# Two graph layers: later loads of x and weights, earlier splits and transposes of x

## The chip, the core and the metric

The kernel runs on one core of a Trainium2 chip. A core has five engines that run their own instruction queues and wait for each other on semaphores: TensorE (PE, matrix products), VectorE (DVE), ScalarE (ACT), GpSimd (POOL) and SyncE (SP). Data come from memory over 16 DMA engines; POOL and SP issue these loads into a queue each. The metric is the device time in microseconds.

## What is computed

Two layers over the same 4096 x 4096 graph, whose entries are 0 or 1 with about 16 ones in a row, and 64 features:

```python
# layer 0
rank = cumsum(adj, axis=1); deg = rank[:, -1:]
k = minimum(deg, 100); pos = rank - (deg - k)
w = adj * where(pos > 0, 0.5 ** (k - pos), 0)
x = layernorm(x + w @ (x @ W0) + b0)
# layer 1
deg = maximum(sum(adj, axis=1) + 1, 1)
h = (adj @ x + x) / deg
z = relu(concatenate([x, h], axis=1) @ W + b1)      # W holds wx over wn
x = layernorm(x + z / maximum(norm(z), 1e-12))
```

Layer 0 needs, for each edge, how many edges stand to its right in its row: the weight halves with every one.

## The kernel before

**Tiles and steps.** The adjacency matrix lies transposed and is cut into 64 tiles (8 row groups g of 512 rows, 8 column pieces k of 512). `load_next` (L102 to L110) issues the load of one tile on POOL's queue, with a cast to bf16. The kernel calls it 8 times ahead of the loop and once in every step of it. A step i handles one tile, groups in order and pieces from 7 down to 0 within a group. PE counts ones by column quarters (`count`, L317; the first count of a tile is the first use of its load), DVE adds these to the counts of the pieces to the right (`cs`), PE spreads them (`spread`), ACT makes `near` of it. `weigh` (L343) then makes the 2^-rank weights by 32 small products (L351, L360) and two evictions, one by ACT (L367) and one by DVE (L368). `gather` (L373) multiplies the weights of the step before with x. The count in step i is that of tile i + 1. Sums of layer 1 over parts of x that are ready fill the later steps (L387).

**x comes twice.** `load_xp` (L122) loads x in an order that fits the tiles into the buffer `c1` (named c in the profile), in two halves: first pieces 4 to 7, then 0 to 3. `split_x` (L218) makes of piece k a high part in fp16 (by POOL, for pieces 6 and 7 by ACT) and a rest, and `split_x_low` (L225, DVE) turns the rest into the low part. `gather` reads both. For groups 2 to 6, `early_px` (L281) transposes these parts on PE, `early_xT` (L286) copies them out by ACT, and `early_pu` (L291) multiplies them with `wc_parts`. `load_x` (L126) loads x of one group in its natural order, 128 KB, and `add_b0` (L308, on POOL) adds the bias b0 to it.

**Weights.** `load_weights` (L211) loads one tile of 385 columns. Of the columns come, on POOL and PE: `prepare` (scales W0), `centered` (wx with its mean taken off, L244), `centered_parts` (L252, makes `wc_parts`), `products`, `prepare_wx`, `prepare_wn`.

**What sets the order.** The order of instructions on each engine is that of the program; no scheduler moves them. Small jobs are put on hooks: `at(i, engine, fn)` (L608) puts a job into step i, after a look into the table `PLACES` (L39), which can give another step. In step i the loop (L711 to L749) runs the jobs of ACT, then `load_next`, then those of POOL, then the tile's work, and at the end those of PE and of DVE. Jobs of one step and engine run in the order in which they were put on the hook. For this change these matter: split_x of piece k stood in the step of tile (0, k); load_weights in step 1 on DVE; load_x and add_b0 of group 0 in steps 3 and 7 on POOL; prepare in step 5, bias_columns in step 7, centered_parts in step 9 on POOL; early_px in steps 3 to 7; early_pu from step 9 on PE.

**Loads that wait on purpose.** `load_x` and `load_weights` first set one column of their target to 0 with a memset on POOL or DVE. The load, on SP's queue, has to wait for this memset; so it is issued only when that engine has come to this point. SP serves its queue in order.

**Start.** PE runs 14 products on zeros (L693) and some more on the first tile (`warm`, L696). Meanwhile DVE makes masks out of number patterns that POOL writes with iota.

Of the kernel before, what the change touches and what calls it, by code (L numbers as in the profile page):

```python
# [10 lines left out]
BF16 = mybir.dt.bfloat16  # L11
# [4 lines left out]
ALU = mybir.AluOpType  # L16
AX = mybir.AxisListType
PE = mybir.EngineType.PE
ACT = mybir.EngineType.Activation
DVE = mybir.EngineType.DVE  # L20
POOL = mybir.EngineType.Pool
SP = mybir.EngineType.SP

P = 128
# [3 lines left out]
Q = P // 4  # L28
MAX_NEIGH = 100
STEP = 128.0  # L30
# [7 lines left out]
HALVED = range(2, 7)  # L38
PLACES = {"centered_parts": (9, POOL), "prepare": (5, POOL), "bias_columns": (7, POOL), "prepare_wx": (10, POOL), "half_c1_b1 3": (38, POOL), "half_c1_b1 4": (46, POOL), "half_c1_b1 5": (57, POOL), "half_c1_b1 6": (62, POOL), "products_parts": (10, POOL), "first_mv 0": (10, "DVE, early"), "first_r 0": (11, "DVE, early"), "first_least 0": (13, "DVE, early"), "first_s 0": (11, ACT), "first_pu 0": (16, PE), "times_degree 0": (18, POOL), "first_least 1": (20, DVE), "first_pu 1": (24, PE), "first_mv 2": (28, DVE), "first_s 2": (29, ACT), "first_r 2": (29, DVE), "half_scale 2": (29, DVE), "first_x1 2": (30, POOL), "first_hi 2": (31, ACT), "first_xl 2": (31, POOL), "first_lo 2": (32, ACT), "first_least 2": (31, DVE), "half_high 2": (26, ACT), "half_rest 2": (26, DVE), "half_degree_out 2": (26, DVE), "half_degree 2": (26, PE), "half_low 2": (27, ACT), "half_pz 2": (27, PE), "half_y 2": (27, DVE), "first_x1 3": (37, POOL), "first_hi 3": (38, "ACT, late"), "first_least 3": (38, "DVE, early"), "half_low 3": (34, ACT), "half_b1 3": (38, POOL), "half_c1 3": (37, POOL), "first_s 4": (44, ACT), "half_scale 4": (45, "DVE, early"), "first_xl 4": (46, POOL), "first_least 4": (45, DVE), "first_lo 4": (47, "ACT, late"), "half_low 4": (42, ACT), "half_b1 4": (46, POOL), "first_s 5": (52, ACT), "half_scale 5": (53, DVE), "first_hi 5": (54, "ACT, late"), "first_least 5": (57, DVE), "half_low 5": (50, ACT), "half_b1 5": (52, POOL), "half_c1 5": (55, POOL), "first_s 6": (60, ACT), "first_xl 6": (62, POOL), "first_lo 6": (62, "ACT, late"), "half_low 6": (58, ACT)}  # L39
LAG = 1  # L40
SAVED = (15, 17, 18, 21, 27)


@with_exitstack
def adj_resnorm_kernel(
# [23 lines left out]
    nc = tc.nc  # L69
    D = x.shape[2]  # L70
    NG, NK = adjT.shape[0], adjT.shape[1]
# [4 lines left out]
    const = ctx.enter_context(tc.tile_pool(name="const", bufs=1))  # L76
# [13 lines left out]
    for g in range(NG):  # L90
        sizes = {3: [1, 1, 2, 2, 2], 4: [2, 2, 2, 2], 7: [2, 2, 4]}.get(g, [1] * 8 if g < 3 else [4, 4])
        k = NK
# [4 lines left out]
    when = {s: i for i, s in enumerate(steps)}  # L97
# [4 lines left out]
    def load_next(n=1):  # L102
        for _ in range(n):
            s = next(loads, None)
            if s is None:
                return
            g, k = s
            a = a16p.tile([P, KB, R], BF16, tag="a16", name=f"a16_{g}_{k}")
            nc.gpsimd.dma_start(out=a, in_=adjT[g, k])  # L109
            A[g][k] = a  # L110
# [5 lines left out]
    c1 = const.tile([P, NB, D], F32, name="c1")  # L116
    xp = c1
# [3 lines left out]

    def load_xp(k0, k1):  # L122
        bs = slice(k0 * KB, k1 * KB)
        nc.sync.dma_start(out=xp[:, bs, :], in_=x_quads[:, bs, :])

    def load_x(g):  # L126
# [3 lines left out]

    load_xp(NK // 2, NK)
    load_next()
    load_xp(0, NK // 2)
    dist = epi.tile([P, P], I32, tag="hT", name="dist")
    nc.gpsimd.iota(dist, [[1, P]], base=0, channel_multiplier=-1)
    load_next()
# [3 lines left out]
    of_m = epi.tile([P, P], I32, tag="z", name="of_m")  # L140
    nc.gpsimd.iota(of_m, [[1, 4], [4 * KB, NK], [4, KB]], base=0, channel_multiplier=-1)
    load_next(6)

    idle = epi.tile([P, R], BF16, tag="near", name="idle")
    nc.vector.memset(idle, 0.0)
# [2 lines left out]
    quarters = [slice(e * Q, (e + 1) * Q) for e in range(4)]  # L148
# [10 lines left out]
    ident = epi.tile([P, P], F32, tag="near", name="ident")  # L159
    nc.vector.tensor_scalar(ident, dist, 0.0, None, ALU.is_equal)  # L160
    cen, wcf, b0T = prep[0:D, 0:D], prep[0:D, D : 2 * D], prep[0:D, 2 * D : 4 * D]
    w32, wc32 = prep[:, 4 * D : 6 * D], prep[:, 6 * D : 7 * D]
    nc.vector.tensor_scalar(cen, ident[0:D, 0:D], -1.0 / D, None, ALU.add)


    has = epi.tile([P, P], BF16, tag="y", name="has")
    nc.vector.tensor_scalar(has, of_p, 0.0, None, ALU.is_equal)
    past = epi.tile([P, P], BF16, tag="hT", name="past")
# [9 lines left out]
        else:  # L178
            nc.vector.tensor_scalar(mine[quarters[e]], one_hot, STEP, None, ALU.mult)

    tri = const.tile([P, Q], BF16, name="tri")
    for rows in quarters:
        nc.vector.tensor_scalar(tri[rows], dist[rows, rows], 0.0, -STEP, ALU.is_lt, ALU.mult)
        nc.vector.scalar_tensor_tensor(
            tri[rows], ident[rows, rows], STEP * MAX_NEIGH, tri[rows], ALU.mult, ALU.add
        )
    most = const.tile([P, 1], F32, name="most")
    nc.vector.memset(most, MAX_NEIGH)
    less = const.tile([P, 1], F32, name="less")
# [1 line left out]


    wts = const.tile([P, 6 * D + 1], F32, name="wts")
    w0_sb, wn_sb, wx_sb, b1_sb, b0_sb, w0T_sb = [wts[:, j * D : (j + 1) * D] for j in range(6)]
    wc_parts = const.tile([P, 2, D], FP16, name="wc_parts")
    wz_parts = const.tile([P, 2, 2 * D], FP16, name="wz_parts")
    b0c = const.tile([P, D], F32, name="b0c")
# [6 lines left out]
    nc.vector.memset(power, -0.5)  # L204
    x1T = const.tile([P, R], FP16, name="x1T")
    ident16 = const.tile([P, P], FP16, name="ident16")
    nc.vector.tensor_copy(ident16, ident)
    ident_b = const.tile([P, P], BF16, name="ident_b")
    nc.vector.tensor_copy(ident_b, ident)

    def load_weights():  # L211

        nc.vector.memset(wts[:, 0:1], 0.0)
        nc.sync.dma_start(out=wts, in_=weights)

    xrs = {}

# [38 lines left out]
        nc.gpsimd.tensor_tensor(wc_parts[:, 1, :], wc32, wc_parts[:, 0, :], ALU.subtract)  # L256

    def bias_columns():
        nc.gpsimd.tensor_copy(b0T, wts[0:D, 6 * D : 6 * D + 1].to_broadcast([D, P]))

    def products():
        pw[1] = ps_m.tile([P, 2, D], F32, tag="m", name="pw_1")
# [133 lines left out]
    def ready(i, g, b):  # L396
        k = b // KB
        return i >= low_at[k] + LAG and i >= when[g, k]

# [75 lines left out]
    def first_hT(g):  # L475
        h = ep["hT", g] = epi.tile([P, R], F32, tag="hT", name=f"hT0_{g}")
        nc.scalar.copy(h, acc0[g])
# [130 lines left out]
    def at(i, engine, fn, *args):  # L608
        i, engine = PLACES.get(" ".join([fn.__name__, *map(str, args)]), (i, engine))
        hooks[i, engine].append((fn, args))  # L610

    def run(i, engine):
        for fn, args in hooks.pop((i, engine), []):
            fn(*args)

    def all_at(i, *work):
        for step, engine, fn, *args in work:
            at(i + step, engine, fn, *args)

    for k in range(NK):  # L620
        i = when[0, k]
        at(i, POOL, split_x, k)
        at(i, DVE, split_x_low, k)
    at(1, DVE, load_weights)
    at(NK - 2, POOL, prepare)
    at(NK + 1, POOL, prepare_wx)
    at(NK + 2, POOL, prepare_wn)
    for g in range(NG):
        at(NK * g + 3, POOL, load_x, g)
        at(NK * g + 7, POOL, add_b0, g)  # L630
        at(min(NK * g + 12, NS - 2), POOL, add_self, g)
    if HALVED:
        all_at(
# [7 lines left out]
            (2, POOL, products_parts),  # L641
        )
    for j, g in enumerate(reversed(HALVED)):
        all_at(j + 3, (0, PE, early_px, g), (1, ACT, early_xT, g))
        all_at(NK + 1 + j, (0, PE, early_pu, g), (0, DVE, early_xw, g))
    for g in range(NG - 1):
        i = NK * (g + 1)
# [42 lines left out]


    pi = ps_a.tile([P, R], F32, tag="acc1", name="pi")
    for i in range(14):  # L693
        nc.tensor.matmul(pi, lhsT=idle[:, 0:P], rhs=idle, start=True, stop=True)

    def warm(n):  # L696

        a = A[0][NK - 1][:, 0, :]
        for i in range(n):
            nc.tensor.matmul(pi, lhsT=a[:, 0:P], rhs=a, start=True, stop=True)  # L700
# [3 lines left out]
    further = const.tile([P, P], BF16, name="further")  # L704
    nc.vector.tensor_copy(further, pf)
    count(0, NK - 1, True, True)
    warm(4)
    spread(0, NK - 1)
    warm(2)
    held = None  # L710
    for c, chunk in enumerate(chunks):  # L711
        ahead = chunks[c + 1] if c + 1 < len(chunks) else []

        shares = [[]] * (len(chunk) - 1) + [ahead]
        nr = near[chunk[0][0]]
        for (g, k), share in zip(chunk, shares):
            i = when[g, k]
            run(i, ACT)
            load_next()
            run(i, POOL)  # L720

            w = weigh(g, k, nr) if i == 0 else None
            for s in share:
                count(*s, s == ahead[0], s == ahead[-1])
            run(i, "DVE, early")
            w = w or weigh(g, k, nr)
            run(i, "ACT, late")
            if i == 0:
                warm(4)
            n_todo = len(todo)  # L730
            done = some_sums(i, 0 if i in SAVED else QUOTA)
            half = 0
            if share and share[-1] == ahead[-1]:
                if held is not None and len(todo) == n_todo:

                    half = KB // 2
                    gather(*held, 0, half)
                spread(*ahead[-1])
            if i == 0:
                warm(3)  # L740
            if done is not None:
                evict_part(done)
            if held is not None:
                gather(*held, half)
            held = (g, k, w)
            if g > 0 and k == NK - 1:
                first_hT(g - 1)
            run(i, PE)
            run(i, DVE)  # L749
# [318 lines left out]
```

## Time and profile before

| what | value |
|---|---|
| median of 3 runs | 234.12 us (233.64 to 234.18) |
| the profiled execution | 233.72 us |
| its span, first to last instruction | 231.7 us |
| PE busy | 209.5 us, 90% |
| DVE busy | 182.2 us, 79% |
| ACT busy | 140.6 us, 61% |
| POOL busy | 112.3 us, 48% |
| adjacency tiles on POOL's queue | 64, 512 KB written each |
| landing of a tile after its issue, median | 15.2 us |
| the first tile: issue, first count | 1.23 us, 8.94 us |
| weights: issue on SP | 18.57 us |
| first natural piece of x: issue on SP | 20.80 us |
| first product with wc_parts | 38.21 us |

```profile
PE   7589999998998999999999999999999999999910
...
PEclk9799999999999999999999999999999999999975
DMA  6999999999999999999999999999970000000013
```

Each digit is the busy share of one of 40 slices of the span, 5.8 us each, in tenths. PEclk is the clock that TensorE was granted, in tenths of full speed. The DMA engines are full from the second slice to the thirtieth (174 us); after that PE works off what is loaded, and the last slices are small operations and stores. A line of the timeline has start, length, engine, source line, operation, output and inputs, and in brackets how long the engine stood idle before it and what ended that.

### The profile page before, as it was taken

The numbers are of one execution on the slowest core, as the hardware profiler recorded it, in microseconds if no ns is written. First come the engines' busy times: TensorE is split into PE (matmuls) and PEld (weight loads), VectorE is DVE, ScalarE is ACT, GpSimd is POOL, SyncE is SP. The second block draws the span as 40 slices with busy tenths as digits, with TensorE's granted clock in tenths as the row PEclk, the third lists the DMA queues.
The fourth block names the chain that finished last, engine by engine and source line by source line (L and its number), as shares of the span: only waits on it lengthen the run. The fifth ranks groups of instructions, "written<-read, shape, count | busy, mean of one in ns | idle before, by whom it ended". The sixth has DMA issues, their size and how long they took to land.

```text
span 231.7 us, 7494 instructions
## 1 busy us (share of the span) xinstructions
PE 209.5 (90%) x3138; PEld 95.2 (41%) x3178; DVE 182.2 (79%) x454; ACT 140.6 (61%) x212; POOL 112.3 (48%) x211
## 2 busy tenths in 40 slices
PE   7589999998998999999999999999999999999910
PEld 2133445443533443334333433443334344776810
DVE  6459877997797789798975996687678866599983
ACT  6057886687778767686557455664675451142684
POOL 7439677761537081641584056325433040079970
PEclk9799999999999999999999999999999999999975
DMA  6999999999999999999999999999970000000013
GB/s 201 209 213 219 215 216 213 217 217 214 215 219 212 214 214 223 211 214 214 218 217 207 200 183 210 204 195 181 205 168 4 3 0 0 3 0 1 23 45 113
DMA packets 11984, 37.36 MB, mean 161 GB/s; under 512 B 1328, under 2 KB 3504, under 8 KB 11952
## 3 DMA queue, kind: packets, MB, share of 16 engines
q0 software_dynamic: 9216, 33.56, 73.7%
q1 hardware_dynamic: 2736, 3.34, 4.7%
q8 instruction: 24, 0.39, 0.6%
q14 instruction: 8, 0.07, 0.1%
HBM read 69.40 MB, written 1.05 MB: 304 GB/s over the span
## 4 chain that ended last, share of the span: by engine, by line
PE 40%; DVE 11%; POOL 4%; ACT 3%; issue 2%; ACTq 0%; DVEq 0%; POOLq 0%
PE acc L378 12%; PE acc_part L387 11%; PE v L351 5%; PE cnt L321 3%; PE v L360 3%; ACT u L961 2%; POOL scratch L947 2%; DVE w L368 2%; POOL scratch L978 2%; DVE cs L331 1%; PE rep L339 1%; PE va L930 1%; PE pz L505 1%; PE vb L387 1%; DVE part L403 1%
## 5 line engine op out<-in xcount | busy, mean ns | idle before, releaser
L367 ACT ACTIVATE w<-v,less 128x1024 int16<-128x1024 f32 x64 | 71.3, 1113 | 43.7 <-PE v L360 31.7
L368 DVE TENSOR_SCALAR w<-v 128x1024 int16<-128x1024 f32 x64 | 78.2, 1221 | 13.0 <-PE v L360 12.1
L378 PE MATMUL acc<-w,xhl 128*128 128x512 bf16 x235 | 65.2, 380 | 1.9 <-issue 1.1
L109 POOL DMA_DIRECT2D a<-in_adjT_dram x64 | 36.9, 622 | 48.2 <-PE acc_part L387 25.4
L387 PE MATMUL acc_part<-a,x1hl 128*128 128x512 bf16 x140 | 38.2, 381 | 1.8 <-issue 1.3
L378 PEld LDWEIGHTS <-xhl 128*128 128x128 f16 x256 | 23.1, 98 | 33.6 <-issue 9.7
L341 ACT ACTIVATE near<-rep,most 128x512 bf16<-128x512 f32 x40 | 27.3, 682 | 8.7 <-PE rep L339 8.6
L387 PEld LDWEIGHTS <-x1hl 128*128 128x128 f16 x224 | 18.6, 98 | 31.1 <-issue 13.3
L351 PE MATMUL v<-a,tri 32*32 32x512 bf16 x1024 | 29.6, 384 | 0.3 <-DVE w L368 0.2
L360 PE MATMUL v<-near,mine 32*32 32x512 bf16 x1024 | 28.1, 376 | 0.0
L331 DVE TENSOR_TENSOR cs<-cnt,cs 128x512 bf16<-128x512 f32 x32 | 21.9, 686 | 4.4 <-PE cnt L321 4.0
L321 PE MATMUL cnt<-a,pick 128*32 128x512 bf16 x256 | 21.4, 389 | 4.2 <-DMA a<-in_adjT_dram 2.9
L351 PEld LDWEIGHTS <-tri 32*32 32x32 bf16 x1024 | 9.5, 87 | 21.7 <-issue 21.5
L339 PE MATMUL rep<-cs,further 128*128 128x512 bf16 x40 | 15.4, 385 | 1.5 <-DVE cs L331 1.1
L565 POOL TENSOR_SCALAR x<-y,mv_l,r_l 128x64 f32<-128x64 f32 x16 | 9.1, 575 | 12.4 <-DVE dr L516 6.4
L947 POOL TENSOR_TENSOR scratch<-scratch,power 128x4 f32<-128x4 f32 (+1 forms) x5 | 6.4, 1279 | 15.2 <-DVE scratch L949 15.1
L306 POOL TENSOR_TENSOR a<-a,ident_b 128x128 bf16<-128x128 bf16 x32 | 12.7, 431 | 0.1
L321 PEld LDWEIGHTS <-pick 128*32 128x32 bf16 x256 | 5.9, 94 | 14.8 <-issue 11.3
L333 DVE CAST cs<-cnt 128x512 bf16<-128x512 f32 x8 | 5.5, 692 | 7.8 <-PE cnt L321 7.8
L360 PEld LDWEIGHTS <-mine 32*32 32x32 bf16 x1024 | 10.2, 87 | 2.8 <-issue 2.4
L961 ACT ACTIVATE u<-u,scratch 128x64 f32<-128x64 f32 x27 | 9.8, 428 | 2.2 <-POOL scratch L980 2.1
L944 ACT ACTIVATE u<-u 128x256 f32<-128x256 f32 (+1 forms) x5 | 2.5, 502 | 12.1 <-DVE u L933 12.1
(177 smaller groups left out, 272.2 us busy)
## 6 DMA issues: line engine op xcount, KB each, us to landing
a<-in_adjT_dram POOLq DMA_DIRECT2D x64, 512.0 KB, 15.2
c<-in_x_quads_dram SPq DMA_DIRECT2D x2, 512.0 KB, 4.5
x<-in_x_dram SPq DMA_DIRECT2D x8, 128.0 KB, 7.2
out_dram<-u SPq DMA_DIRECT2D x8, 128.0 KB, 1.7
wts<-in_weights_dram SPq DMA_DIRECT2D x1, 192.5 KB, 7.2
```

The costliest lines, as they stand in the source:

```text
L109: nc.gpsimd.dma_start(out=a, in_=adjT[g, k])
L321: nc.tensor.matmul(cnt[g][quarters[q], :], lhsT=pick[:, PW - 4 * k : PW - 4 * k + Q], rhs=A[g][k][:, q, :], start=first, stop=last,)
L331: nc.vector.tensor_tensor(new, cnt[g], cs[g], ALU.add)
L339: nc.tensor.matmul(pr, lhsT=further, rhs=cs[g], start=True, stop=True)
L341: nc.scalar.activation(near[g], pr, AF.Relu, bias=most, scale=-1.0)
L351: nc.tensor.matmul(v[e // 2][quarters[q], e % 2, :], lhsT=tri[quarters[e], :], rhs=A[g][k][quarters[e], q, :], start=True, stop=False,)
L360: nc.tensor.matmul(v[e // 2][quarters[q], e % 2, :], lhsT=mine[quarters[e], 4 * k + q, :], rhs=nr[quarters[e], :], start=False, stop=True,)
L367: nc.scalar.activation(w[:, 0:2, :], v[0], AF.Relu, bias=less)
L368: nc.vector.tensor_scalar(w[:, 2:4, :], v[1], -STEP * MAX_NEIGH, 0.0, ALU.add, ALU.max)
L378: nc.tensor.matmul(acc0[g], lhsT=xhl[:, b, :], rhs=w[:, q, :].bitcast(BF16), start=(k, q) == (NK - 1, 0), stop=(k, q) == (0, KB - 1),)
L387: nc.tensor.matmul(acc, lhsT=x1hl[:, b, :], rhs=A[g][b // KB][:, b % KB, :], start=first, stop=last)
L961: nc.scalar.activation(o[:, t, :], y[:, t, :], AF.Identity, bias=off[:, t : t + 1], scale=r[:, t : t + 1])
```

## The change

It moves loads to later points and some jobs to earlier ones. The second half of x is no longer issued right after the first tile, but after the eighth, behind a memset on POOL. The weights are loaded in two parts; their columns are put in another order, so that W0, wx, W0 transposed and the column of b0 come first (193 columns, step 1), and wn, b1 and b0 later (192 columns, step 6). load_x of group 0 goes from step 3 to step 7, its add_b0 from step 7 to step 9. split_x and split_x_low stand one step sooner (piece 7 stays in step 0). early_px and early_xT stand two steps sooner. On DVE, `tri` is made ahead of `has` and `past`, and `ident16`, `ident_b` and `cen` only after the first counts. Twelve products on zeros instead of 14.

Apart from these, no engine's order changes. In the changed order of POOL, the add_b0 of group 0 stands directly ahead of centered_parts; in SP's order the second part of the weights stands directly ahead of the first load_x.

```diff
+WARM = 12, 4, 2, 4, 3
...
     def load_xp(k0, k1):
         bs = slice(k0 * KB, k1 * KB)
+        if k0 == 0:
+            nc.gpsimd.memset(xp[:, 0, 0:1], 0.0)
         nc.sync.dma_start(out=xp[:, bs, :], in_=x_quads[:, bs, :])
...
     load_xp(NK // 2, NK)
     load_next()
-    load_xp(0, NK // 2)
...
     load_next(6)
+    load_xp(0, NK // 2)
...
-    nc.vector.tensor_scalar(cen, ident[0:D, 0:D], -1.0 / D, None, ALU.add)
...
-    w0_sb, wn_sb, wx_sb, b1_sb, b0_sb, w0T_sb = [wts[:, j * D : (j + 1) * D] for j in range(6)]
+    w0_sb, wx_sb, w0T_sb, wn_sb, b1_sb, b0_sb = [wts[:, n : n + D] for n in (0, D, 2 * D, 3 * D + 1, 4 * D + 1, 5 * D + 1)]
...
-    nc.vector.tensor_copy(ident16, ident)
...
-    nc.vector.tensor_copy(ident_b, ident)
...
-    def load_weights():
+    def load_weights(c0, c1):
...
-        nc.vector.memset(wts[:, 0:1], 0.0)
-        nc.sync.dma_start(out=wts, in_=weights)
+        nc.vector.memset(wts[:, c0 : c0 + 1], 0.0)
+        nc.sync.dma_start(out=wts[:, c0:c1], in_=weights[:, c0:c1])
...
     for k in range(NK):
-        i = when[0, k]
+        i = max(when[0, k] - 1, 0)
         at(i, POOL, split_x, k)
         at(i, DVE, split_x_low, k)
-    at(1, DVE, load_weights)
+    at(1, DVE, load_weights, 0, 3 * D + 1)
+    at(6, DVE, load_weights, 3 * D + 1, 6 * D + 1)
...
-        at(NK * g + 3, POOL, load_x, g)
-        at(NK * g + 7, POOL, add_b0, g)
+        at(NK * g + 3 if g else 7, POOL, load_x, g)
+        at(NK * g + 7 if g else 9, POOL, add_b0, g)
...
-        all_at(j + 3, (0, PE, early_px, g), (1, ACT, early_xT, g))
+        all_at(j + 1, (0, PE, early_px, g), (1, ACT, early_xT, g))
...
-    for i in range(14):
+    for i in range(WARM[0]):
...
     spread(0, NK - 1)
-    warm(2)
+    warm(WARM[2])
+    nc.vector.tensor_copy(ident16, ident)
+    nc.vector.tensor_copy(ident_b, ident)
+    nc.vector.tensor_scalar(cen, ident[0:D, 0:D], -1.0 / D, None, ALU.add)
```

Left out of the diff are the move of the block that makes `tri`, the host's new order of the weight columns, the column of b0 in `bias_columns`, and the numbers of `warm`, which stay 4, 2, 4 and 3.

## The prediction

> **What bounds the kernel now.** I read the page first (TensorE, PE below, busy 90% of the span; the DMA row full in 30 of 40 slices), then the timeline of the first 46 us, then the landing of every adjacency tile against the matmul that first needs it. Tile n is the n-th load of L109; step i weighs tile i and counts tile i+1.
>
> ```profile
> 8.94 0.62 PE L321 MATMUL cnt<-a,pick 128*32 128x512 bf16 x4 [2.67 <-DMA a<-in_adjT_dram]
> ...
> 27.88 0.40 PE L321 MATMUL cnt<-a,pick 128*32 128x512 bf16 x4 [0.27 <-DMA a<-in_adjT_dram]
> ...
> 29.07 1.23 DVE L368 TENSOR_SCALAR w<-v 128x1024 int16<-128x1024 f32 x1
> ...
> 30.21 0.28 DVE L226 TENSOR_SCALAR xhl<-xr 128x256 f16<-128x256 f32 x1
> 30.21 0.86 POOL L311 TENSOR_TENSOR x<-x,wts 128x256 f32<-128x256 f32 x1
> ...
> 33.88 0.39 POOL L253 TENSOR_SCALAR prep<-prep 64x64 f32<-64x64 f32 x1
> ...
> 35.10 0.31 POOL L256 TENSOR_TENSOR wc_parts<-prep,wc_parts 128x64 f16<-128x64 f32 x1
> ```
>
> ```profile
> 38.21 0.40 PE L295 MATMUL eu<-wc_parts,xT 128*128 128x64 f16 x8
> ```
>
> In this timeline PE waits for a DMA twice: for tile 0 (8.94) and for tile 7 (27.88). From tile 1 to tile 8 the tiles land about 2.4 us apart and more where other loads mix in, PE takes about 2.3 us a step, and so it catches up. Landing and first use are: tile 6 24.98 and 25.21, tile 7 27.81 and 27.88, tile 8 30.58 and 30.75, tile 10 35.58 and 35.88. Later PE falls behind the loads (2 to 6 us of slack), with one exception: tile 43 lands at 119.38 and is used at 119.45. Everywhere else until 220 us the bound is PE itself with its dependencies on DVE (VectorE): the windows from 60 to 210 us show it 93 to 99% busy. A delay at step 9 therefore goes to the end, and a lead at step 9 does not, since tile 43 takes it back.
>
> The rows of POOL (GpSimd) show what this change touches. add_b0 of group 0 (L311) runs at 30.21, in step 7, and centered_parts (L253 to L256, 33.88 to 35.41) in step 9; at 38.21, at the end of step 9, PE reads their result wc_parts.
>
> ```profile
> x<-in_x_dram SPq DMA_DIRECT2D x8, 128.0 KB, 7.2
> out_dram<-u SPq DMA_DIRECT2D x8, 128.0 KB, 1.7
> wts<-in_weights_dram SPq DMA_DIRECT2D x1, 192.5 KB, 7.2
> ```
>
> These issue rows give the price of a load: 128 KB take 1.7 us when nothing else moves (the stores at the end), but 7.2 us beside the stream of tiles.
>
> **The change, part by part.**
>
> *Second half of x.* 512 KB leave the head of the queues. By the packet records each of the 16 DMA engines sends its first packet of tile 0 right after its last packet of x (4.98 to 6.04 us); the first half of x ends at 3.71 to 4.22. Tile 0 so lands some 1.5 us sooner, at about 7.4. Not shown is whether its descriptors are ready that early; at worst it starts at 4.98 as now, a gain of nothing to 0.5. The half itself is now issued after POOL's six tile issues (end at 7.71) and one memset (0.1); at 11.2 its packets begin (+3.4 us, as for every later load), it lands near 16 and is needed at step 3 (POOL at 17 to 19). The bytes before tile 3 are the same, so tiles 3 and on gain nothing. On the path: zero.
>
> *Start-up order.* Two warming matmuls fewer (0.43 us each), PE free at 5.8 instead of 6.3: hidden before tile 0. The mask tri moves ahead of has, past and mine on DVE; all end near 6.7, ahead of the first count. ident16, ident_b and cen (0.23, 0.22 and 1.25) move behind the first cast of the counts, into the 2.85 us in which DVE waited before its first w. Without that cover they would cost 1.7.
>
> *Splits one step, transposes two steps sooner.* Same instructions. ACT (ScalarE) casts twice at step 0, so w is 0.1 to 0.4 later, read 2.7 us after (gather at 16.89). Transposes (PE 0.39, ACT 0.59 a step) leave steps 6 and 7 for steps 1 and 2. Since tile 7 sets step 6, this too ends in the wait for a DMA: zero.
>
> *Weights in two parts.* One memset (0.06) and one issue on SP (0.33) more. The second part (Wn, b1, b0) is issued at the end of step 6, behind DVE's w and the low split of piece 0. Tile 7 gains: of the first x piece some three quarters are out of its way (a 1 KB packet stretches the 305 ns between an engine's tile packets to 359, so 8 x 54 ns x 0.75 = 0.3) and half of the weights (8 x 30 ns = 0.25). It lands at 27.25. DVE's row at 29.07 moves to 28.5, its w ends at 29.7, the low split at 29.9: the second part is issued at **30.0**, where all of it was issued at 18.57.
>
> *First x piece from step 3 to step 7.* POOL's memset is ready at about 27.5, but the SP queue is served in order and the weights' second part stands ahead: issue at 30.3 instead of 20.80.
>
> *add_b0 of group 0 from step 7 to step 9.* Here is the added wait. add_b0 needs both new loads; in POOL's order it now stands **ahead of** centered_parts, and behind that stand wx_parts, wn, wz_parts and the next tile issues. When do both loads land? By row: weights and x piece before went through one after another, weights issued at 18.57, the piece landed at 20.80 + 8.6 = 29.4, thus 10.8 us for 16 packets on each engine; with the smaller first part 10.6. So the piece lands at 30.0 + 10.6 = 40.6. Then add_b0 0.86, centered_parts 35.41 - 33.88 = 1.53: wc_parts at 43.0, and PE's first eu at 43.05 where it was 38.21: **+4.85 us**. Ends: if the piece came together with the weights' part (30.0 + 7.2 = 37.2) eu would start at 39.65, +1.4; if each took the 8.6 us of the slowest and then queued 3, +5.9. I take 4.85, as the pair of before is the same pair.
>
> A rule against the row: the Trainium skill, "DMA: Bandwidth & Descriptors", section Specifications, gives about 0.6 us to the first byte on SP's path, and some 27 GiB/s to each of 16 engines, an estimate of about 1 us for 128 KB. With it both loads would lie there by 32, before POOL reaches add_b0 at some 33.9, and this part would cost nothing. The rows under load say 6.2 to 8.6 for all eight pieces; I go by these. The same page's section on queues, rings and completion order (the engines serve their rings in turn, packet by packet) says why: a small load shares with 324 ns tile packets.
>
> *TensorE's clock.* PE stands from about 37.6 to 43. What does that do to the granted clock?
>
> ```profile
> 6.00:9.00 3.00, 0.33 (x6) 0.15 (x4) 1.62 (x12) 0.00 (x0) 1.71 (x4) 0.89 1.07 210
> 9.00:12.00 3.00, 3.00 (x11) 0.93 (x10) 0.69 (x1) 0.16 (x1) 0.54 (x1) 0.54 1.07 214
> ```
>
> After 2.7 us of waiting for tile 0 the clock (third number from the right) fell to a half for 3.4 us. The skill's "TensorE: Matmul & The Clock Gate" (Part 1) asks for an idle window of about 3.4 us; the trace shows a shorter wait doing it. Either way 5.4 us suffice here; by the rule alone a stall under 3.4 would be free of it, by the trace not. Its price: nothing at least; 1.7 at most (half of 3.4 us). In steps 10 to 12 PE's streams fill about 2.2 of 2.7 us, so at half clock a step takes some 4.0 and 3.4 us lose a third: **+1.1**.
>
> **Sum.** 4.85 + 1.1 = 5.95. Nothing gives it back: tile buffers hold tiles to 17, landed by 53, and with PE late tile 43's wait vanishes. The profiled execution took 233.7 (span 231.7 and 2.0 around it), so 239.7; it lies 0.4 under the median 234.1, which I leave to the range.
>
> **Rivals.**
> 1. *The stall without the clock's loss* (DVE paces steps 10 to 12 anyway; for: DVE is 98% busy from 40 to 50; against: it idles with PE in the stall): 233.7 + 4.85 = 238.6. Chance 0.2.
> 2. *Half hidden*: the piece lands with the weights, because packets of 768 bytes take less: +1.4 and no clock loss, 235.1. Against: the pair of before. Chance 0.11.
> 3. *No stall, not slower*: the loads land before POOL's tile issue of step 9 ends (33.9), as the skill's figure would have it. Deciding point: the piece has landed by about 35, since add_b0 and centered_parts then end by PE's arrival at 37.6. Then PE leads by 0.6 from tile 7, but tile 43 leaves 0.1: 233.6. For: POOL has slack before 38.21; against: no load beside the stream took less than 6.2 us. Chance 0.09, of which 0.03 for a lead that is kept (233.0).
> 4. *Worse*: the clock stays low for two windows and POOL's backlog delays x1: 242. Chance 0.05.
>
> The forecast has 0.55. A difference below 0.3%, 0.7 us, can't be told from none here. Slower: 0.55 + 0.2 + 0.11 + 0.05 = 0.91; within 0.06; faster 0.03. The range takes in forecast, rival 1 and the bounds of the stall in part: 236.3 to 241.4.
>
> **What would show it.** In the changed profile: the first wait for tile 0 ends near 7.4; DMA landing of the second part of the weights 7, of the first x piece about 10 us after issue at 30; L310 (add_b0) waiting for a DMA near 40; PE idle some 5 us before its first eu, near 43, with a granted clock below 1 after it; and the last store about 6 us later. I am wrong if add_b0 starts before 36, if PE makes up the delay before 119 us, or if the second part of the weights leaves well before 30.

## The result and the profile after

| | before | changed |
|---|---|---|
| median, measured side by side (4 runs each) | 233.95 us (233.64 to 234.18) | 240.25 us (239.79 to 240.63) |
| ratio, 95% interval | | 1.0269 (1.0245 to 1.0294) |
| span of the profiled execution | 231.7 us | 238.0 us |
| PE busy | 209.5 us | 214.8 us |
| first count, of tile 0 | 8.94 us | 8.85 us |
| weights: issue, first part and second part | 18.57 us, one load | 17.68 and 30.37 us |
| first natural piece of x: issue, landing | 20.80 and 29.4 us | 30.74 and 40.84 us |
| first product with wc_parts (eu) | 38.21 us | 42.78 us |
| tile 43: landing, first count | 119.4, 119.45 us | 121.3, 125.96 us |

The changed kernel is 2.7% slower; the profiled execution is the fastest of its four, at 239.79 us. Two rows of its page, PE's busy tenths and the clock that PE was granted, 5.95 us a slice, and two of its DMA issues:

```profile
PE   8689993799999999999999999999999999999920
...
PEclk9999999599999999999999999999999999999995
...
x<-in_x_dram SPq DMA_DIRECT2D x8, 128.0 KB, 6.9
...
wts<-in_weights_dram SPq DMA_DIRECT2D x1, 96.0 KB, 7.6
```

In the row of before, no slice of PE from the third to the last but two is under 8. Here two are, the seventh and eighth (36 to 48 us), with 3 and 7 tenths, and the clock of the eighth is 5. The first dip of the clock, in before's second slice, is gone. So the loss sits in one place. The timeline of that place in the changed kernel (start, length, engine, line, operation, in brackets the idle time before it and what ended that):

```profile
30.37 0.33 SPq L213 DMA_DIRECT2D wts<-in_weights_dram  x1
...
30.74 17.77 SPq L131 DMA_DIRECT2D x<-in_x_dram  x2
...
41.01 0.63 POOL L310 TENSOR_TENSOR x<-x,wts 128x256 f32<-128x256 f32 x1 [7.62 <-DMA x<-in_x_dram]
...
42.78 0.21 PE L294 MATMUL eu<-wc_parts,xT 128*128 128x64 f16 x1 [4.72 <-POOL wc_parts L254]
...
42.82 0.30 POOL L255 TENSOR_TENSOR wc_parts<-prep,wc_parts 128x64 f16<-128x64 f32 x1
...
43.17 0.53 PE L294 MATMUL eu<-wc_parts,xT 128*128 128x64 f16 x7 [0.18 <-POOL wc_parts L255]
```

Read it from the bottom up. PE stood 4.72 us until POOL gave it the first half of wc_parts. POOL had stood 7.62 us ahead of add_b0 (L310), until the piece of x had landed. The piece was issued at 30.74 (the row joins it with the next group's load, hence its 17.77), right behind the second part of the weights. The windows that follow the stall (stretch and length, busy us of PE, PE's weight loads, DVE, ACT and POOL with counts, then the granted clock, the DMA share and GB/s):

```profile
40.00:43.00 3.00, 0.21 (x1) 0.10 (x1) 0.00 (x0) 0.00 (x0) 1.75 (x5) 0.69 1.09 218
43.00:46.00 3.00, 2.83 (x23) 2.40 (x22) 0.77 (x3) 0.00 (x0) 2.57 (x8) 0.50 1.04 209
46.00:49.00 3.00, 3.00 (x53) 1.20 (x49) 2.74 (x12) 1.71 (x3) 2.76 (x8) 0.67 1.07 216
```

PE is at half clock from 41.15 to 47.98 us: 6.8 us, 5.2 of them after PE has work again. Meanwhile the DMA engines go on (1.04 to 1.09), so the loads pile up and no later tile is waited for: tile 11 is counted 7.4 us after it landed, tile 43 still 4.6 us after.

### The profile page after: what moved, and what is told of

Same layout as the page of the kernel before. It is cut to its first block, busy times and chain, and to the rows that moved or that the text cites. A ratio compares the mean times of both kernels' runs of the same rounds, so it can differ in the third digit from the quotient of the medians.

```text
span 238.0 us, 7537 instructions
## 1 busy us (share of the span) xinstructions
PE 214.8 (90%) x3176; PEld 96.0 (40%) x3176; DVE 182.7 (77%) x455; ACT 140.5 (59%) x212; POOL 110.8 (47%) x212
## 4 chain that ended last, share of the span: by engine, by line
PE 42%; DVE 9%; POOL 4%; ACT 2%; issue 1%; ACTq 0%; DVEq 0%; POOLq 0%
PE acc L377 12%; PE acc_part L386 11%; PE v L350 5%; PE cnt L320 3%; PE v L359 3%; ACT u L964 2%; PE vb L386 2%; POOL scratch L950 2%; DVE w L367 2%; POOL scratch L981 1%; DVE cs L330 1%; PE rep L338 1%; PE va L933 1%; PE va L386 1%; PE ma L386 1%
## 5 line engine op out<-in xcount | busy, mean ns | idle before, releaser
L367 DVE TENSOR_SCALAR w<-v 128x1024 int16<-128x1024 f32 x64 | 78.1, 1221 | 11.1 <-PE v L359 10.2
L377 PE MATMUL acc<-w,xhl 128*128 128x512 bf16 x256 | 69.8, 382 | 0.0
L110 POOL DMA_DIRECT2D a<-in_adjT_dram x64 | 36.4, 581 | 49.0 <-PE acc_part L386 25.8
L386 PE MATMUL acc_part<-a,x1hl 128*128 128x512 bf16 x156 | 40.4, 382 | 0.1
L377 PEld LDWEIGHTS <-xhl 128*128 128x128 f16 x256 | 23.2, 98 | 34.7 <-issue 10.8
L350 PE MATMUL v<-a,tri 32*32 32x512 bf16 x1024 | 29.4, 388 | 0.1
```

The source lines that it names most:

```text
L350: nc.tensor.matmul(v[e // 2][quarters[q], e % 2, :], lhsT=tri[quarters[e], :], rhs=A[g][k][quarters[e], q, :], start=True, stop=False,)
L367: nc.vector.tensor_scalar(w[:, 2:4, :], v[1], -STEP * MAX_NEIGH, 0.0, ALU.add, ALU.max)
L377: nc.tensor.matmul(acc0[g], lhsT=xhl[:, b, :], rhs=w[:, q, :].bitcast(BF16), start=(k, q) == (NK - 1, 0), stop=(k, q) == (0, KB - 1),)
L386: nc.tensor.matmul(acc, lhsT=x1hl[:, b, :], rhs=A[g][b // KB][:, b % KB, :], start=first, stop=last)
```

## The experiments

Ten kernels and the changed one once more, most of them on two theories. **Mine**: the late loads hold add_b0, add_b0 holds centered_parts behind it on POOL, that holds PE, and the idle PE loses its clock. **The rival**: the loss comes from the other edits (order of the start, splits and transposes sooner, half of x late). A second question is whether the lower clock costs anything, or DVE paces those steps anyway.

### Loads early again: everything else of the change kept

```diff
-    at(6, DVE, load_weights, 3 * D + 1, 6 * D + 1)
+    at(2, DVE, load_weights, 3 * D + 1, 6 * D + 1)
-        at(NK * g + 3 if g else 7, POOL, load_x, g)
+        at(NK * g + 3, POOL, load_x, g)
```

> The changed kernel with only the two late loads put back to early steps: the second part of the weights in step 2, x of group 0 in step 3; add_b0 of group 0 stays in step 9, and all other edits stay. Late loads as the cause: both loads land by about 30 us, POOL never waits for them, the first eu starts near 38 us, no drop of the granted clock at 41 us, time 233.6 to 234.4. Other edits as the cause (start-up order, splits and transposes sooner, half of x late, add_b0 in step 9): about 240, unchanged.

Measured: 234.51 us against 233.81, ratio 1.0027 (1.0012 to 1.0041). The loads land at 29.8 and 32.6, eu starts at 38.35, the clock is full at 41. All but 0.7 us of the 6.3 are gone with these two lines.

### The late loads alone, on the kernel before

```diff
-    at(1, DVE, load_weights)
+    at(1, DVE, load_weights, 0, 3 * D + 1)
+    at(6, DVE, load_weights, 3 * D + 1, 6 * D + 1)
-        at(NK * g + 3, POOL, load_x, g)
-        at(NK * g + 7, POOL, add_b0, g)
+        at(NK * g + 3 if g else 7, POOL, load_x, g)
+        at(NK * g + 7 if g else 9, POOL, add_b0, g)
```

> The kernel before with only the late loads: weights in two parts (steps 1 and 6), x of group 0 in step 7, add_b0 of group 0 in step 9; x whole at the head, splits and transposes where they were. Late loads as the cause: add_b0 waits until about 41 us, first eu near 43, clock at a half after it, time 239.5 to 241. Other edits as the cause: about 234.

Measured: 240.26 us, ratio 1.0271 (1.0231 to 1.0310), the time of the whole change. Its timeline repeats the stall:

```profile
40.73 0.63 POOL L311 TENSOR_TENSOR x<-x,wts 128x256 f32<-128x256 f32 x1 [7.58 <-DMA x<-in_x_dram]
...
42.49 0.21 PE L295 MATMUL eu<-wc_parts,xT 128*128 128x64 f16 x1 [4.49 <-POOL wc_parts L255]
```

With the run before it, the rival theory falls from both sides: the late loads suffice for the loss, and without them nearly all of it is gone.

### One load early, the other late

The changed kernel with only the second part of the weights back in step 2:

> The changed kernel with only the second part of the weights put back to step 2; x of group 0 is still loaded in step 7. This tells the queueing of two loads from the lateness of each. If the piece of x is late only because it stands behind the weights' part: it is issued near 28 us, lands near 35.5, eu near 38 to 38.5, time 233.8 to 234.5. If the piece is late by itself (it takes 10 us anyway): lands at 38 to 39, eu near 40.5, time 236 to 237. Other edits as the cause: 240.

and with only the piece of x back in step 3:

> The changed kernel with only the load of x of group 0 put back to step 3; the second part of the weights stays in step 6. It is issued at 30 and takes 7 to 7.6 us: lands at 37.3 to 38, then add_b0 and centered_parts, eu near 39.8 (+1.6 us against before). PE then waits about 2 us. If a wait of that length does not halve the clock: time about 235.6; if it does: 237 to 237.5. Other edits as the cause: 240.

Measured: 235.55 us, ratio 1.0072 (1.0052 to 1.0092), and 236.77 us, ratio 1.0106 (1.0066 to 1.0146). First the timeline with the weights early, then that with x early:

```profile
29.31 0.33 SPq L131 DMA_DIRECT2D x<-in_x_dram  x1
...
37.27 0.63 POOL L310 TENSOR_TENSOR x<-x,wts 128x256 f32<-128x256 f32 x1 [3.29 <-DMA x<-in_x_dram]
...
39.04 0.19 PE L294 MATMUL eu<-wc_parts,xT 128*128 128x64 f16 x1 [0.44 <-POOL wc_parts L254]
```

```profile
30.89 0.33 SPq L213 DMA_DIRECT2D wts<-in_weights_dram  x1
...
38.91 0.63 POOL L310 TENSOR_TENSOR x<-x,wts 128x256 f32<-128x256 f32 x1 [5.01 <-DMA wts<-in_weights_dram]
...
40.68 0.19 PE L294 MATMUL eu<-wc_parts,xT 128*128 128x64 f16 x1 [2.09 <-POOL wc_parts L254]
```

Each load alone takes 7.8 and 7.9 us; behind the weights the piece takes 10.1. So the queue of two is worth 40.84 - 37.1 = 3.7 us, 1.4 of it the later issue and 2.3 the longer landing. The packet records show this queue: alone, the piece's first packet moves 3.4 us after the issue; behind the weights it moves 5.8 us after (at 36.54), when the first engines are done with the weights' packets (33.75 to 37.3). Alone, a late piece moves eu by 0.8 us and late weights by 2.5 us; my expectations had 0 to 0.3 and 1.6, since the issues came 1.3 and 0.9 us later than I had them and the landings took some 0.3 us longer. Both late loads matter, then, and most of all together. The fourth run's stall of only 2.1 us was followed by one stretch of half clock (42.0 to 45.4 us). Of the two branches of that expectation, the one where the clock halves (237 to 237.5) is the nearer to the median; but the profiled execution, at 238.05 us, is the slowest of its five runs and does not stand for the others.

### The same late loads, but add_b0 behind what PE waits for

Order on POOL in step 9: centered_parts, prepare_wx, prepare_wn, products_parts, and only then add_b0 of group 0. Both loads stay as late as in the change.

```diff
             (1, POOL, centered_parts),
+            (3, POOL, prepare_wx),
+            (3, POOL, prepare_wn),
...
             (2, POOL, products_parts),
+            (3, POOL, add_b0, 0),
```

> The changed kernel with both loads as late as it has them, but the wait put elsewhere: in POOL's order add_b0 of group 0 stands behind centered_parts, wx_parts, the scaling of Wn and wz_parts (the last three move from step 10 to step 9 for this) instead of ahead of them. If the loads cost time by what is queued behind the waiting add_b0: the first eu runs near 38 us without a stall; add_b0 ends near 41.5 and VectorE's y of group 0, due at 39.7, waits for it, about 1.9 us; time 235.5 to 237. If the late loads cost time in another way (memory traffic, late tiles): still about 240.

Measured: 236.16 us, ratio 1.0104 (1.0085 to 1.0123).

```profile
37.77 0.40 PE L294 MATMUL eu<-wc_parts,xT 128*128 128x64 f16 x8
...
40.82 0.64 POOL L310 TENSOR_TENSOR x<-x,wts 128x256 f32<-128x256 f32 x1 [0.58 <-DMA x<-in_x_dram]
...
41.49 0.42 DVE L543 TENSOR_TENSOR y<-pz,x 128x256 f32<-128x256 f32 x1 [2.81 <-POOL x L310]
...
42.63 0.38 PE L338 MATMUL rep<-cs,further 128*128 128x512 bf16 x1 [2.02 <-DVE cs L330]
```

The loads land when they did (the piece at 40.7), yet eu runs at 37.77 without a stall. So not the traffic costs the time, but what stands behind the wait. The wait moves to DVE: y comes at 41.49 instead of 39.71, cs behind it, and PE's rep behind that. 1.8 us of lateness and one stretch of half clock (43.95 to 47.36 us) account for the 2.46 us over before (236.16 - 233.70).

### Keeping PE busy through the stall

```diff
+        if g == HALVED[-1]:
+            fill = early_bank([P, R], F32, "fill")
+            for i in range(21):
+                nc.tensor.matmul(fill, lhsT=some[:, 0:P], rhs=some[:, 0:R], start=True, stop=True)
```

`some` is the mask `mine`, flattened.

> The changed kernel with 21 extra matmuls of 128x512 on PE, results unused, ahead of the first eu; at full clock they take 21 x 0.21 = 4.5 us and fill the stall from 37.9 to about 42.4, so that PE works while it waits. If the lower granted clock after the stall costs time: no slices at half clock, eu still near 42.8, and the time falls to about 238.2 (240.2 less 1.9). If VectorE sets the pace of those steps and the lower clock is free: 240.2.

Measured: 238.64 us, ratio 1.0219 (1.0202 to 1.0236).

```profile
PEclk9999999999999999999999999999999999999985
```

```profile
37.48 4.70 PE L295 MATMUL fill<-mine 128*128 128x512 bf16 x20
...
42.48 0.19 PE L299 MATMUL eu<-wc_parts,xT 128*128 128x64 f16 x1 [0.31 <-POOL wc_parts L254]
```

The stall is the same, the clock stays full, and the excess over before falls from 6.30 us (240.25 - 233.95) to 4.94 (238.64 - 233.70). The lower clock costs 1.36 us; the rest is the stall. This is a difference of medians: the four runs of the changed kernel had granted clocks of 0.953 to 0.974 over the whole span, so not all had the same low time.

### The other edits

Only the second half of x late, on the kernel before:

> The kernel before with only the second half of x moved behind the eighth tile's issue. Late half worth nothing, as forecast: 233.5 to 234.5, tile 0 used near 8.85, as in the changed kernel, and not at 7.4. If a lead does survive to the end: 233.0 or less. If the half costs something: 234.6 or more.

Only what is neither a late load nor the late add_b0 (start order, warming products, splits and transposes, weights in two early parts):

> The changed kernel without its three late loads and without the late add_b0: x whole at the head, weights in two parts in steps 1 and 2, x of group 0 in step 3, add_b0 of group 0 in step 7. What stays is the start-up order of VectorE, two warming matmuls fewer, splits one step and transposes two steps sooner. If these are free: 233.5 to 234.4. If the 0.3% that the first experiment left over come from these: 234.5 or more.

Measured: 234.20 us, ratio 1.0011 (0.9995 to 1.0028), and 233.78 us, ratio 1.0003 (0.9992 to 1.0014). Both are no difference that can be told from none. The 0.3% of the first experiment do not come from the start order or the splits. Whether the late half and the late add_b0 share them is open: the profiled execution of that experiment was no longer than before's (span 231.6).

### Can the idea be made to pay?

With add_b0 behind centered_parts, wx_parts and Wn, a late piece of x hurts no one if it lands before y needs it. Two attempts on the kernel before load x of group 0 in step 8 and in step 7. Both also move x of group 4 from step 35 to step 38, behind tile 43.

```diff
-        at(NK * g + 3, POOL, load_x, g)
-        at(NK * g + 7, POOL, add_b0, g)
+        at({0: 8, 4: 38}.get(g, NK * g + 3), POOL, load_x, g)
+        if g:
+            at(41 if g == 4 else NK * g + 7, POOL, add_b0, g)
...
+            (3, POOL, prepare_wx),
+            (3, POOL, prepare_wn),
+            (3, POOL, add_b0, 0),
```

> An attempt to beat the kernel before, built on it: x of group 0 is loaded in step 8 and lands about 38 us, behind tile 10; its add_b0 stands behind centered_parts, wx_parts and Wn on POOL (step 9), so only VectorE's y (due at 39.7) needs it; x of group 4 is loaded in step 38 instead of 35, behind tile 43, its add_b0 in step 41. If tiles 7 to 10 and tile 43 are the only places where loads set the pace: a lead of 0.2 to 0.4 us at tile 10 survives tile 43, and the time is 233.3 to 233.7, at most 0.2% under the kernel before. If y waits: 234 to 235. If another tile takes the lead back: no difference.

> As the last attempt to beat the kernel before, with x of group 0 one step sooner (step 7): issued near 28.8 us, landed near 36.5, so that y at 39.4 no longer waits for POOL, where it waited 1.28 us. If that wait was what took the lead back: PE is 0.1 to 0.3 us ahead of the kernel before at tiles 10 to 13 and still at tile 43, time 233.2 to 233.6. If the piece now sits in front of tile 10 and takes the lead there: no difference from the kernel before.

Measured: 233.84 us, ratio 0.9998 (0.9983 to 1.0012), and 233.49 us, ratio 0.9995 (0.9980 to 1.0010). Step 8 was too late: tile 10 was counted at 35.57, 0.31 sooner than before, but y waited 1.28 us for the piece, and at tile 12 PE was 0.34 behind. With step 7 POOL still waits for the piece, but y no longer waits for POOL:

```profile
38.28 0.73 POOL L311 TENSOR_TENSOR x<-x,wts 128x256 f32<-128x256 f32 x1 [1.52 <-DMA x<-in_x_dram]
...
39.35 0.42 DVE L544 TENSOR_TENSOR y<-pz,x 128x256 f32<-128x256 f32 x1 [0.59 <-PE pz L539]
```

PE is 0.35 us ahead of before at tiles 10 to 13 and 0.17 ahead at tile 43, which now lands at 119.0 (before 119.4). The other half of the lead goes at tile 14, not at tile 43. 0.2 us are less than the measurement can tell, so this is no faster version that I could show.

### The changed kernel a second time

> The changed kernel itself, a second profiled execution. If the start of the first one (tile 0 used at 8.85, clock full from 9 to 12 us) and the 6.8 us of half clock after the stall belong to the program, both come again; if they hang on the phase of the clock's windows, the start or the length of the low clock differs while the stall at the first eu is again 4.5 to 4.8 us and the time again 239.8 to 240.7.

Measured: 241.09 us, one run. The stall is again 4.65 us and eu is at 42.84. But the clock differs at both places: it is low after tile 0, where it was full in the first execution, and after the stall it is low for 10.2 us instead of 6.8 (windows as above, the clock third from the right):

```profile
40.00:43.00 3.00, 0.16 (x1) 0.10 (x1) 0.00 (x0) 0.00 (x0) 1.70 (x5) 0.54 1.08 218
43.00:46.00 3.00, 2.82 (x24) 2.40 (x22) 0.71 (x2) 0.00 (x0) 2.57 (x8) 0.50 1.03 208
46.00:49.00 3.00, 2.67 (x40) 0.93 (x38) 2.79 (x12) 1.46 (x2) 2.76 (x8) 0.50 1.06 213
49.00:52.00 3.00, 2.95 (x49) 1.29 (x49) 1.88 (x7) 1.34 (x3) 1.30 (x5) 0.75 1.09 221
```

So the length of the half clock does not belong to the program alone, and one more low stretch fits the 241.09, a single run.

## Why the prediction was right, point by point

**The mechanism was right, step for step.** Loads in a row on SP, add_b0 held, centered_parts held behind it, PE idle at its first eu, the clock down after it, and no later place that gives the time back. Taking the loads away, adding them alone, and moving the wait to another engine each gave the time that this chain asks for, the first of them to 0.7 us.

| step | predicted | measured |
|---|---|---|
| second part of the weights issued | 30.0 us | 30.37 |
| piece of x issued, landed | 30.3, 40.6 us | 30.74, 40.84 |
| first eu | 43.05 (+4.85) | 42.78 (+4.57) |
| from first eu to tile 43's count, beyond before's 81.24 us: at full clock | 0 | 0.56 (fill experiment: 81.80) |
| the same: the clock | +1.1 | +1.38 (83.18 - 81.80) |
| sum at tile 43 | +5.95 | +6.51 |
| span | +5.95 | +6.3 |

**Three terms were mis-sized.** eu came 0.27 us sooner than I had it: add_b0 took 0.63 and not 0.86, and PE starts as soon as the first half of wc_parts is there (42.78). But the other seven products need the second half and start only at 43.17, so about 0.4 of the 0.56 is time that the first eu did not show. The other 0.2 come at tile 14: in the fill experiment PE waits 0.30 us there for DVE's w (50.40). And the clock: I had one stretch of 3.4 us at 1.1. It was 6.8 us, of which PE had work in 5.2, and they cost some 1.4. My step of 4.0 us at half clock does not follow from 2.2 us of streams, which doubled make 4.4, but it came out: with the late loads alone tile 11 to tile 12 takes 4.1 us (45.19 to 49.27), where before took 2.33. What I lacked is that the next step gives some of it back (tile 12 to 13 takes 2.33 there and 2.89 before). So the low time was longer than I had it and cheaper for its length, and the two errors partly cancel; that the sum missed by only 0.6 us is in part luck.

**The clock, by stretch.** Half-clock time in the windows of seven executions, with the idle time of PE ahead of it:

| execution | wait for tile 0, low after it | wait at first eu, low after it | first eu to tile 43's count |
|---|---|---|---|
| before | 2.67, 3.4 us | none | 81.24 us |
| fill | 1.41, none | 0.31, none | 81.80 |
| weights early | 2.93, 3.4 us | 0.44, none | 81.91 |
| x early | 2.82, 6.8 us | 2.09, 3.4 us | 82.56 |
| changed | 2.27, none | 4.72, 6.8 us | 83.18 |
| late loads alone | 2.74, none | 4.49, 6.8 us | 83.72 |
| changed again | 2.57, 3.4 us | 4.65, 10.2 us | 84.11 |

Against the two rows with a broken eu and full clock (about 81.85), one low stretch costs 0.7 us, two cost 1.3 and 1.9, three 2.3. What counts is the low time in which PE has work: 3.4, 5.2, 6.5 and 7.6 us in these four, thus 0.2 to 0.3 us lost for each us. Rival 1, the stall without the clock's loss at 238.6, is the time that the fill experiment made (238.64), so DVE alone does not pace these steps; but a PE that streams without a pause would lose half of the 5.2 us, 2.6, and about half of that was hidden (an estimate). Rival 4 named two low stretches, and they came, but cost 1.38 us and did not make it 242.

**The rule on the idle window.** I went by the trace, where a wait of 2.7 us had been enough, and not by a rule that asks for an idle 3.4 us. The runs agree that less is enough: after 2.09 us the clock halved. They also show that the length does not decide it: 2.74 us at the start left it full, 1.99 us (in the attempt with step 8) did not. What decides is where the idle time falls. In each trace all changes of the clock lie on a grid of 3.41 us, whose phase differs from run to run. Here is the grid's window over each of these two waits, first of the attempt with step 8, whose clock halved at the end of it, then of the late loads alone, whose clock stayed full:

```profile
6.30:9.71 3.41, 1.42 (x11) 0.59 (x10) 1.69 (x11) 0.00 (x0) 1.93 (x4) 1.00 1.06 210
```

```profile
4.66:8.07 3.41, 1.47 (x8) 0.64 (x7) 3.12 (x16) 0.13 (x1) 2.98 (x6) 1.00 1.08 238
```

PE was busy for 1.42 and for 1.47 us of 3.41, 42% and 43%. Counted from the first change of the clock that each records, the thirteen traces have 825 such windows that began at full clock. In 26, the end of the kernel included, PE was busy 42% or less, and after each of these the clock halved; after none of the others did it. In the changed kernel the window up to 41.15 us had 9%. When the full clock comes back these shares do not tell: a low window with 83% was enough in one trace, one with 100% was not in another.

**Rivals 2 and 3.** The piece did not land with the weights (40.84 against 37.94), and neither load was there by 35. The figure for an idle path, about 1 us for such a load, is 6 to 9 us short beside the stream of tiles.

**What was wrong: tile 0 at 7.4 us.** I had the second half of x out of its way and tile 0 sooner by 1.5 us. It landed at 8.8, 0.1 sooner. In seven other executions with the half late it lands between 7.9 and 9.0, in five with it at the head between 8.8 and 9.0. The windows from 4 to 6 us, first of before, then of the changed kernel:

```profile
4.00:6.00 2.00, 2.00 (x8) 0.78 (x7) 1.93 (x6) 0.79 (x1) 2.00 (x4) 1.00 1.06 313
```

```profile
4.00:6.00 2.00, 2.00 (x6) 0.76 (x5) 1.82 (x10) 0.78 (x1) 2.00 (x5) 1.00 0.97 154
```

The engines are booked as busy in both (1.06 and 0.97), but move 313 GB/s with x and 154 without. Most of that is the mix: a packet of 4096 bytes occupies an engine for a median of 159 ns when it is of x (172 in the changed kernel), and for 324 ns when it is of a tile, in the whole run; the full stream later moves some 214 GB/s at 1.06. The packets of tile 0 do start sooner, the first at 4.18 us (before 4.98). But in the changed kernel six of them take 1.5 to 1.7 us each. In all seven executions with the half late that land tile 0 at 8.7 to 9.0, four to eight packets take 0.9 to 2.2 us; in the fill experiment one does, and tile 0 lands at 7.9. The end I had named at worst, a gain of nothing to 0.5, is what came here; why these packets are slow I did not settle.

PE was not free sooner either (6.58 us, before 6.27): the twelve warming products took 0.44 us each and the fourteen of before 0.36. That costs nothing ahead of tile 0. The half itself, now between the tiles, makes tiles 2 and 3 land 1.2 us later (15.0 and 17.5 against 13.9 and 16.3), where I had tiles 3 and on unchanged. Tile 7 landed at 27.7 and not at 27.25. That all this is worth nothing at the end was right (ratio 1.0011 for the half alone): PE meets the loads again at tile 7.

**Tile 43 as a cap.** Right in the place, and its price fits: with x of group 4 out of its way tile 43 landed some 0.4 us sooner in both attempts, where the 8 packets of 54 ns that I had used make 0.43.

## What to carry to other kernels

Before a load is moved later, ask what stands behind its first reader on that reader's queue: here the piece of x was not urgent, but centered_parts, behind its add_b0, was. Where the load can't come sooner, moving the reader behind the urgent work takes a few lines and gave back 3.8 of 6.3 us here. Beside a stream that fills the DMA engines, the second of two small loads on one queue took 10 us here, where a lone one took 7.8. And a stall of PE costs its length and then, where the clock halves, 0.2 to 0.3 us more for each us of low clock in which PE has work.

## What the runs showed of the hardware

- The half clock comes in whole stretches of about 3.4 us: 3.4, 6.8 or 10.2 us, in the ten of the thirteen profiled executions where it came ahead of the kernel's end. The same program had none after tile 0 in one execution and one stretch in the next, two after the stall and then three. The Trainium skill, "TensorE: Matmul & The Clock Gate", Part 1, says that the window is free-running and the effect differs from run to run; these numbers agree.
- The full clock was lost after each window of 3.41 us in which PE was busy 42% or less (26 windows of 825) and after none with 43% or more, whatever the length of the single wait.
- A load of 128 KB from SP's queue takes 4.7 to 10.8 us while tiles stream; a store of the same size takes 1.7 us when they don't. The second of two loads issued 0.4 us apart takes 10.0 to 10.8 (seven executions) where a lone one at the same place takes 7.8.
- A packet of 4096 bytes of a tile, which is cast on the way, occupies a DMA engine for a median of 324 ns, one of x, which is not cast, for 159 to 172. That the cast is the reason is not shown.
- With the second half of x out of the way, four to eight of tile 0's first packets took 0.9 to 2.2 us in seven of eight executions; with it in front (five executions) none took over 0.6.
